# First layer: another order inside the convolutions' copies, and a PSUM count that starts anew after every merged stretch

## The chip, the cores and the metric

The kernel runs on one core of a Trainium2 chip. The time is device time in microseconds (us) of that core. The engines have short names in what follows: PE is TensorE (matrix products and transposes; PEld its weight loads), DVE is VectorE, ACT is ScalarE, POOL is GpSimd, and SP issues most of the data transfers (DMA). PE writes its results to PSUM, a memory of eight banks of 2 KiB per partition; DVE and ACT read them from there and write to SBUF, the on-chip working memory.

## The reference

The input x is a float32 tensor of shape 8 x 56 x 56 x 192 (image, row, column, channel). Four layers follow one another, each of the form x = x + layer(groupnorm(x)). The last three (a pooled attention with nine-point windows, a gated attention in 8 x 8 windows, and a linear recurrence along rows, columns and diagonals) are not touched by the change. The first layer is:

```python
p = silu(x @ p_w.T + p_b); q = silu(x @ q_w.T + q_b); v = silu(x @ v_w.T + v_b)   # 192 -> 576 channels
qv = q * v
o1 = toeplitz(qv, a1)             # along the columns of each row, per channel
o2 = toeplitz(transpose(qv), a2)  # along the rows of each column, per channel
out = (p * (o1 + o2)) @ o_w.T + o_b
```

A toeplitz product is, for each of the 576 channels, a 56 x 56 matrix built from one sequence of coefficients, applied to each row (or column) of the image.

## The kernel before

`layer0` handles the eight images one after the other. The 576 channels are nine heads of 64, named by s. Two heads make a chunk, named by c: chunks 0 to 3 hold two heads each and chunk 4, the tail, holds one. For one chunk:

- **Gates and products** (`project`, gates at L358, silu at L369): four steps g compute q and v for a quarter of the image each. A step takes two PSUM tiles, or one in the tail chunk. ACT applies silu, and DVE and POOL multiply q and v into the tile `qv` (L381, L387), once row by row and once column by column.
- **Turns** (`turn_both`, L414 and L419; `turn` for the tail head, L433 and L440): PE transposes qv for eight image rows into one PSUM tile. DVE copies one half of it to one operand (`ol`), and after that ACT copies the other half to the other operand (`or`). A pair of heads has seven turns, the tail head four.
- **Convolutions** (`convolve`, L457): two steps q per head. A step runs 32 matrix products, one per channel, whose operands hold both the Toeplitz tables and the turned qv, so that one product gives o1 + o2 for a channel. Its PSUM tile has two banks (k); each holds eight channels (v) of 56 image rows (h), and the partitions hold image columns, for two channel groups at once (u). One copy per step moves it to `ot`, a tile of 120 partitions x 56 rows x 128 channels, by DVE when q is 0 (L477) and by ACT when q is 1 (L475). The tail head has its own two copies (L468).
- **Post** (`post`, for chunks 0 and 1 and for chunks 2 and 3; `post_tail` for chunk 4): computes p, transposes `ot` back (L518), multiplies (L523), applies the output weights (L532, L553, L564) and adds to the image's accumulators `acca` and `accb` (L484, L486). Its tile `o` is taken by name (`outs`), apart from the ring.

PE's order is fixed by the program: the layer opens a manual schedule for PE. The other engines are ordered by the scheduler that builds the program, and each runs its own queue in order.

**The ring of PSUM tiles.** All eight banks belong to tiles of two banks: three tiles with the tag `c` and one with the tag `o`. Every step asks `banks()` for a tile. In wide mode each fourth request, by the running count `ring["at"]`, gets `o` and the others get the next of the three `c`; in narrow mode all requests get `c` and the count stands still. A request must wait until the readers of the tile's previous user are done.

**The loop over chunks.** For each chunk c, `merge` interleaves two lists. One is the previous post (if there is one) or, when there is none, the gates of the first two steps of the next chunk; the other is this chunk's turns. Then the remaining gate steps of the next chunk run, beside steps of group normalization where there are any (`normalize` for the next image at c = 2, `tell` for the finished image at c = 1; their statistics go through PE at L129), and then this chunk's convolutions. In chunk 3 gates and convolutions alternate. The posts therefore fall into the merges of c = 2 and c = 4 (narrow), and the tail's post into that of c = 0 of the next image (wide). After a convolution the tables of the head after next are loaded by DMA into the operand that it has freed (`toeplitz`, L334; in the first image from the freshly built coefficients, later from a stored copy).

Of the kernel before, what the change touches and what calls it, by code (L numbers as in the profile page):

```python
# [17 lines left out]
H = 56  # L18
# [40 lines left out]
def image_dma(queue, dram, xa, xb, store=False):  # L59


    parts = []
    for at in range(0, HW, HQ // 2):
        cols = slice(at, at + HQ // 2)
        parts.append((xa[0:CP, cols], dram[:, 0, cols]))
        parts.append((xa[CP:CA, cols], dram[0 : CA - CP, 1, cols]))
        h, own = at // HQ, slice(at % HQ, at % HQ + HQ // 2)
        parts.append((xb[h * CB : (h + 1) * CB, own], dram[CA - CP :, 1, cols]))
    for s, d in parts:
        if store:  # L70
            queue.dma_start(d, s)
        else:
            queue.dma_start(s, d)
# [104 lines left out]
def layer0(cx, xin, xout, w, consts):  # L178
# [15 lines left out]
    with ExitStack() as es:  # L194
# [7 lines left out]
        ring = {"at": 0, "wide": True}  # L202

        def banks():
            if ring["wide"]:
                ring["at"] += 1
                if ring["at"] % 4 == 0:
                    return cx.tile(psc, [128, 2, 512], "o", bufs=1)
            return cx.tile(psc, [128, 2, 512], "c")
# [17 lines left out]
        def fetch_wqv(q, queue=nc.sync):  # L227
            if q < B * NC:
                wqv[q] = cx.tile(cp, [128, 3, 2, 128], "wqv", bufs=2)
                queue.dma_start(wqv[q], w["w_qv"][q % NC])  # L230

        def fetch_wp(j, queue=nc.sync):
            wps[j] = cx.tile(cp, [128, 3, 2, 128], "wp")
            queue.dma_start(wps[j], w["w_p"][j])
# [8 lines left out]
        with ExitStack() as pes:  # L243
# [22 lines left out]
            for t in (1, 2):  # L266
# [13 lines left out]
                for i in range(3):  # L280
                    ps = banks()[0:32, 0, 0:NP]
# [4 lines left out]
                for s in range(NS):  # L286
                    ps = banks()[0:DS, 0, 0:NP]
# [116 lines left out]
        def turn_both(n):  # L404

            order = (n % 2, 1 - n % 2)

            def step(i0):
                ps = banks()[0:120]
                view = ps.rearrange("p k (d i) -> p k d i", i=8)  # L410
                for i in range(8):
                    for e, k in enumerate(order):
                        rows = slice(e * DS, (e + 1) * DS)
                        nc.tensor.transpose(  # L414
                            view[:, k, :, i], qv[rows, i0 + i, :], ident[rows, rows]
                        )
                for t, rows, copy in zip(both, (T2, T1), (nc.vector.tensor_copy, nc.scalar.copy)):
                    dst = t[rows, :, 0:ND].rearrange("p k (d i) -> p k d i", i=H)
                    copy(dst[:, :, :, i0 : i0 + 8], view[rows])  # L419

            return [lambda i0=i0: step(i0) for i0 in range(0, H, 8)]

        def turn(n):

            s = n % NS
            e = s % 2 * DS
            left, right = pairs[n % 2]

            def step(i0, ni):
                ps = banks()[0:120]  # L430
                view = lambda k: ps[:, k].rearrange("p (d i) -> p d i", i=8)
                for i in range(ni):
                    nc.tensor.transpose(  # L433
                        view(i // 8)[:, :, i % 8], qv[e : e + DS, i0 + i, :],
                        ident[e : e + DS, e : e + DS],
                    )
                src = ps[:, 0 : ni // 8].rearrange("p k (d i) -> p d k i", i=8)
                for t, rows, copy in ((left, T2, nc.vector.tensor_copy), (right, T1, nc.scalar.copy)):
                    dst = channels(t)[rows, :, i0 : i0 + ni].rearrange("p d (k i) -> p d k i", i=8)
                    copy(dst, src[rows])  # L440

            return [lambda i0=i0: step(i0, min(16, H - i0)) for i0 in range(0, H, 16)]

        def convolve(n, ot):


            s = n % NS
            left, right = pairs[n % 2]
            tail = s == NS - 1

            def step(q):
                ps = banks()
                for k in range(2):
                    for v in range(8):
                        for u in range(2):
                            d = q * 16 + 8 * k + v + u * 32
                            nc.tensor.matmul(  # L457
                                ps[u * 64 : (u + 1) * 64, k, v * H : (v + 1) * H],
                                left[:, d * H : d * H + 64],
                                right[:, d * H : (d + 1) * H],  # L460
                                start=True, stop=True, skip_group_check=True,
                            )
                if tail:
                    for u, copy in enumerate((nc.vector.tensor_copy, nc.scalar.copy)):
                        d0 = q * 16 + u * 32
                        dst = ot[0:H, :, d0 : d0 + 16].rearrange("p h (k v) -> p h k v", k=2)
                        src = ps[u * 64 : u * 64 + H, :, 0 : 8 * H]
                        copy(dst, src.rearrange("p k (v h) -> p h k v", h=H))  # L468
                    return
                else:  # L470
                    d0 = s % 4 * 32 + 16 * q
                    dst = ot[:, :, d0 : d0 + 16].rearrange("p h (k v) -> p k v h", k=2)
                    src = ps[0:120, :, 0 : 8 * H].rearrange("p k (v h) -> p k v h", h=H)
                if q % 2:
                    nc.scalar.copy(dst, src)  # L475
                else:
                    nc.vector.tensor_copy(dst, src)  # L477

            return [lambda q=q: step(q) for q in range(2)]

        def add(m, j, x, ps):
# [217 lines left out]
        def merge(a, b):  # L699

            n = max(len(a), len(b))
            for i in range(n):
                for x in (a, b):
                    for f in x[-(-i * len(x) // n) : -(-(i + 1) * len(x) // n)]:
                        f()
# [11 lines left out]
        def whole(steps):  # L717
            return [lambda f=f, h=h: (f(), h()) for f, h in steps]
# [3 lines left out]
        for b in range(B):  # L722
            more = b + 1 < B
            for c in range(NC):
                n = b * NS + 2 * c
                two = c < NC - 1
                turns = turn_both(n) if two else turn(n)

                i = b * NC + c
                fetch_wqv(i + 2)  # L730
                ahead = project(xn if two else nxt, i + 1) if two or more else []
                early = [] if fill else ahead[0:2]
                ring["wide"] = c not in (2, 4)
                merge(fill + [f for f, _ in early], turns)
                ring["wide"] = True
                for _, f in early:
                    f()
                ahead = whole(ahead[len(early) :])
                if fill:
                    fetch_wp({2: 1, 4: 2, 0: 0}[c])  # L740
                fill, beside = [], []
                if c == 0:
                    if after is not None:
                        image_dma(nc.sync, xout[b - 1], *after, store=True)
                        beside, telling = tell(b - 1, *after)
                    if more:
                        nxt = load_raw(b + 1)
                if c == 1:
                    acc = new_acc(b)
                    beside = [lambda f=f: f(banks) for f in telling]  # L750
                if c == 2 and more:
                    beside = normalize(nxt)

                if c % 2 == 0:
                    ot = cx.tile(cp, [120, H, 128] if two else [H, H, DS], "ot")
                convs = []
                for m in (n, n + 1) if two else (n,):
                    *some, last = convolve(m, ot)
                    convs += some + [lambda m=m, last=last: (last(), toeplitz(m + 2))]

                if c == NC - 2:
                    k = len(ahead)
                    ahead = [f for pair in zip(ahead, convs[0:k]) for f in pair]
                    convs = convs[k:]
                merge(ahead, beside)
                for f in convs:
                    f()
                if c in (1, 3):
                    fill = post(c // 2, xn, ot, acc)
            fill, after = post_tail(xn, ot, acc), acc  # L770
            xn = nxt
# [1448 lines left out]
```

## Time and profile before

| what | value |
|---|---|
| median of three runs | 4062.7 us (4059.47 to 4067.02) |
| the profiled execution: its own time | 4071.48 us |
| its span, first to last instruction | 4069.7 us |
| PE busy | 3788.5 us (93%) |
| DVE busy | 2415.4 us (59%) |
| ACT busy | 1843.3 us (45%) |
| POOL busy | 1529.7 us (38%) |
| mean granted clock of PE | 0.98 |
| last PE work of the first layer | 1931 us from the start |

The profile is of one execution. A row of a group of instructions gives line, engine, operation, the tiles written and read, the shapes and a count. A row of the timeline gives the start and the length in us, then the engine, line and tiles; what stands in brackets is the idle time of the engine before it, and the instruction whose end released it. A row of the waits gives who waited for whom: total us, number of times, longest. In a table of stretches each engine has its busy time and its number of instructions, followed by the clock granted to PE (1.00 is full), the share of time that the DMA engines were busy, and GB/s. PE's transposes and products follow each other closely, and their recorded lengths overlap.

### The profile page before, as it was taken

To read this page: it belongs to the slowest core of one execution; us is meant where nothing else is said; L and a number is where in the kernel's file an instruction comes from. 1 tells how busy PE (TensorE), PEld (TensorE's weight loads), DVE (VectorE), ACT (ScalarE), POOL (GpSimd) and SP (SyncE) were. 2 spreads that over 40 slices of the span, in tenths; PEclk is the share of its full clock that TensorE was granted. 3 is DMA by queue.
4 is the path that set the end of the run, shared out by engine and by line. 5 is a ranking of instruction groups with operands and counts; after the bars stand their busy time and mean duration, and the time that the engine had idled before them with its cause. 6 is when DMAs were issued, how large, how long until landed. Compare 5 with 4: busy or idle time off the path is not lost.

```text
span 4069.7 us, 115870 instructions
## 1 busy us (share of the span) xinstructions
PE 3788.5 (93%) x51036; PEld 2658.5 (65%) x51036; DVE 2415.4 (59%) x3318; ACT 1843.3 (45%) x2021; POOL 1529.7 (38%) x1325
## 2 busy tenths in 40 slices
PE   6989999999998999999799999899989999998997
PEld 4777767677776767777466666444435555556997
DVE  5557675666657665565544444566656666664664
ACT  2444444344444434444334443343335555553663
POOL 3222242222233222223433333333334445444776
PEclk9999999999999999999899999999999999999999
DMA  7865353423526352342433443556558766663333
GB/s 154 166 137 145 81 141 103 119 76 102 128 76 158 87 134 68 87 112 65 120 99 99 112 100 102 158 167 204 178 152 189 176 153 161 149 141 101 94 103 98
DMA packets 390300, 507.94 MB, mean 125 GB/s; under 512 B 176932, under 2 KB 326724, under 8 KB 388404
## 3 DMA queue, kind: packets, MB, share of 16 engines
q1 hardware_dynamic: 385621, 494.07, 47.9%
q8 instruction: 401, 6.57, 0.7%
q10 hardware_dynamic: 3135, 3.47, 0.3%
q0 software_dynamic: 1040, 2.99, 0.3%
q14 instruction: 103, 0.84, 0.1%
HBM read 344.69 MB, written 155.65 MB: 123 GB/s over the span
## 4 chain that ended last, share of the span: by engine, by line
PE 68%; DVE 11%; issue 7%; ACT 5%; DMA 4%; POOL 3%; SPq 2%; POOLq 0%; DVEq 0%; ACTq 0%
PE c L358 9%; PE h L2053 6%; PE v L1541 6%; PE c L499 6%; PE o L532 4%; PE c L1060 4%; PE c L457 4%; PE y L1095 3%; PE o L358 3%; PE kv L1601 3%; DVE ol L419 2%; PE c L1066 2%; PE c L1763 2%; PE c L553 2%; PE o L457 1%
## 5 line engine op out<-in xcount | busy, mean ns | idle before, releaser
L387 POOL TENSOR_TENSOR qv<-s,s 128x392 f32<-128x392 f32 (+3 forms) x320 | 574.7, 1824 | 1296.0 <-ACT s L369 1033.9
L358 PE MATMUL c<-x,wqv 64*128 64x392 f32 x2556 | 458.1, 503 | 21.5 <-DVE ot L477 7.0
L358 PEld LDWEIGHTS c<-x,wqv 64*128 64x128 f32 x2556 | 249.7, 190 | 179.6 <-issue 9.6
L369 ACT ACTIVATE s<-c,bqv 128x784 f32<-128x784 f32 (+1 forms) x235 | 213.6, 914 | 258.3 <-PE c L358 240.9
L381 DVE TENSOR_TENSOR qv<-s,s 128x784 f32<-128x784 f32 (+1 forms) x160 | 232.8, 1465 | 128.5 <-ACT s L369 128.5
L499 PE MATMUL c<-x,wp 64*128 64x224 f32 x2688 | 284.1, 357 | 15.3 <-ACT s L506 14.5
L419 DVE COPY ol<-c 56x1024 f32<-56x1024 f32 x183 | 217.5, 1209 | 105.0 <-PE c L414 105.0
L499 PEld LDWEIGHTS c<-x,wp 64*128 64x128 f32 x2688 | 256.2, 190 | 19.8 <-ACT s L506 16.7
L419 ACT COPY or<-c 56x1024 f32<-56x1024 f32 x183 | 182.7, 1008 | 170.9 <-DVE ol L419 164.9
L523 DVE TENSOR_TENSOR s<-s,c 128x896 f32<-128x896 f32 x112 | 121.8, 1088 | 231.3 <-ACT s L506 224.9
L457 PEld LDWEIGHTS c<-or,ol 120*64 120x64 f32 x6912 | 217.0, 143 | 30.8 <-issue 23.3
L457 PE MATMUL c<-or,ol 120*64 120x56 f32 x6912 | 224.5, 227 | 11.5 <-issue 6.7
L1552 ACT ACTIVATE vb<-sm 128x1024 f32<-128x1024 f32 (+1 forms) x100 | 103.9, 1040 | 261.7 <-issue 218.1
L2084 POOL TENSOR_TENSOR y<-y,s 128x448 f32<-128x448 f32 x168 | 185.2, 1103 | 90.1 <-ACT s L2063 90.1
L506 ACT ACTIVATE s<-c,bp 128x448 f32<-128x448 f32 x224 | 129.9, 631 | 179.6 <-PE c L499 178.3
L2053 PE MATMUL h<-ringv,am 128*64 128x57 f32 (+1 forms) x4400 | 192.6, 235 | 17.6 <-DVE ringv L2040 10.6
L1541 PE MATMUL v<-wvb,wa 128*128 128x512 f32 (+1 forms) x400 | 191.9, 612 | 6.1 <-ACT wa L1427 6.1
L2053 PE MATMUL h<-ringh,am 128*64 128x57 f32 (+1 forms) x4400 | 186.1, 231 | 8.1 <-DVE ringh L2059 8.1
L2053 PEld LDWEIGHTS h<-ringv,am 128*64 128x64 f32 x4400 | 168.1, 140 | 20.9 <-DVE ringv L2040 11.5
L358 PE MATMUL o<-x,wqv 64*128 64x392 f32 x900 | 165.2, 497 | 13.2 <-DVE ot L477 2.8
L1060 PE MATMUL c<-wv,xc 128*126 128x192 f32 x896 | 175.7, 339 | 0.5 <-issue 0.5
L2053 PEld LDWEIGHTS h<-ringh,am 128*64 128x64 f32 x4400 | 166.1, 139 | 10.4 <-DVE ringh L2059 10.4
(273 smaller groups left out, 7853.6 us busy)
## 6 DMA issues: line engine op xcount, KB each, us to landing
or<-tt SPq DMA_DIRECT2D x252, 196.0 KB
ol<-tt SPq DMA_DIRECT2D x252, 196.0 KB
vt<-v SPq DMA_DIRECT2D x56, 672.0 KB
v<-vb SPq DMA_DIRECT2D x96, 384.0 KB
x<-x SPq DMA_DIRECT2D x110, 168.0 KB
wqv<-in_l_w_qv SPq DMA_DIRECT2D x38, 384.0 KB
x<-in_x SPq DMA_DIRECT2D x64, 196.0 KB
x<-x SPq DMA_DIRECT2D x110, 112.0 KB
```

The lines of the kernel that those rows point to most:

```text
L358: nc.tensor.matmul(ps[:, h, 0:n], wqv[q][rows, k, i, :], xn[rows, k, g * n : (g + 1) * n], start=(k == 0), stop=(k == 2),)
L369: nc.scalar.activation(t, ps[rows, :, 0:n], AF.Silu, bias=bqv[rows, j : j + 1])
L381: nc.vector.tensor_tensor(sub(qv[rows, 7 * g :, 64 + H - 1 :], (HH * 120, 2), (120, 7), (-1, H)), *(t.rearrange("p u (h w) -> p u h w", w= ...
L387: eng.tensor_tensor(sub(qv[rows, w0:, H - 1 - 7 * g - HH * u :], (120, w1 - w0), (-1, 7)), *(t[:, u].rearrange("p (h w) -> p w h", w=H)[:, ...
L419: copy(dst[:, :, :, i0 : i0 + 8], view[rows])
L457: nc.tensor.matmul(ps[u * 64 : (u + 1) * 64, k, v * H : (v + 1) * H], left[:, d * H : d * H + 64], right[:, d * H : (d + 1) * H], start=Tr ...
L499: nc.tensor.matmul(ps[:, h, u * n : (u + 1) * n], wps[j][rows, k, u, :], xn[rows, k, g * n : (g + 1) * n], start=(u == 0 and k == 0), stop ...
L532: nc.tensor.matmul(outs[q][:, h, i * n : (i + 1) * n], wo[rows, 2 * j + u, 0:CA], gated[g][rows, u, h * n : (h + 1) * n], start=(i == 0 an ...
L1060: nc.tensor.matmul(out(i, u), group(i, u), wv[0], start=(u == 0), stop=True, skip_group_check=True,)
L1541: nc.tensor.matmul(out, x[:, at : at + n], wt, start=(k == 0), stop=(k == 1), skip_group_check=True,)
L2053: nc.tensor.matmul(ps[sides[c], y], am[a][:, m * CB : (m + 1) * CB], old[:, x], start=(n < 2), stop=True, skip_group_check=True,)
L2084: nc.gpsimd.tensor_tensor(v, v, line[:, j], ALU.add)
```

## The change

Two edits, both in the first layer.

In `convolve`, the copy from PSUM to `ot` of the heads other than the tail visits the same 896 elements per partition in another order. Before, the order from outside to inside was bank k, channel v, image row h: the innermost step goes through consecutive words of PSUM and through `ot` in steps of a whole row of 128 channels. Now it is h, k, v: the innermost 16 elements are consecutive words of `ot`, and PSUM is read in steps of 56 words. The dimension that the code names h is the outer one, and the 16 channels are the inner ones, as in the tail's copies.

In the loop over chunks, the line behind `merge` put the ring back into wide mode. Now it sets the running count to zero as well, so that the next three requests get `c` and the fourth gets `o`. The line stands in the loop over all chunks and so runs behind each merge.

```diff
                     d0 = s % 4 * 32 + 16 * q
-                    dst = ot[:, :, d0 : d0 + 16].rearrange("p h (k v) -> p k v h", k=2)
-                    src = ps[0:120, :, 0 : 8 * H].rearrange("p k (v h) -> p k v h", h=H)
+                    dst = ot[:, :, d0 : d0 + 16].rearrange("p h (k v) -> p h k v", k=2)
+                    src = ps[0:120, :, 0 : 8 * H].rearrange("p k (v h) -> p h k v", h=H)
...
                 ring["wide"] = c not in (2, 4)
                 merge(fill + [f for f, _ in early], turns)
-                ring["wide"] = True
+                ring.update(at=0, wide=True)
```

## The prediction

> **What bounds the kernel now.** I read the page first (busy rows, chain), then the stretches of the first layer, which ends near 1931 us, and then every wait of TensorE (PE) there. The chain that ended last is 68% PE. A steady image (990 to 1220 us) keeps PE busy 214.9 of 230 us, VectorE (DVE) 148.8 and ScalarE (ACT) 106.9, so an edit counts only through PE's 15 idle us per image.
>
> The view of one line's instructions gives the edited copies (L475, L477), and the last head's copies (L468), which already go columns outside, channels inside (ns: min/median/max):
>
> ```profile
> L475 ACT COPY ot<-c x48: 1653/1737/1826, 95.5 to 1875.7; 120x896 f32<-120x896 f32 x48
> L477 DVE COPY ot<-c x49: 1633/1711/1792, 97.4 to 1876.6; 120x896 f32<-120x896 f32 x49
> L468 DVE COPY ot<-c x11: 1071/1075/1083, 297.4 to 1918.6; 56x896 f32<-56x896 f32 x11
> L468 ACT COPY ot<-c x11: 902/902/904, 298.5 to 1919.7; 56x896 f32<-56x896 f32 x11
> ```
>
> Same 896 elements per partition, two thirds and half of the time. Whom PE waits for in the first layer (total us, times, longest):
>
> ```profile
> PE c L358 <- DVE ot L477: 7.0, 5, 1.4
> PE o L358 <- DVE ot L477: 2.8, 2, 1.4
> PE o L358 <- DVE acca L484: 2.5, 2, 1.3
> PE o L358 <- DVE acca L486: 2.4, 2, 1.2
> ```
>
> The first two rows are all that the edited copies cost PE directly, bar 1.3 us at L518. The last two are what a restart right behind a post can remove.
>
> **Part 1, the copies.** 128 of them, half on each engine. From the L468 row I take 1.08 us on DVE (saves 0.64) and 0.90 on ACT (saves 0.84): 41 us of DVE and 53 of ACT. Almost all lies beside PE work. In the timeline where chunk 3 begins:
>
> ```profile
> 1147.49 3.17 DVE L477 COPY ot<-c 120x896 f32<-120x896 f32 x2
> 1149.18 2.25 PE L358 MATMUL c<-x,wqv 64*128 64x392 f32 x12 [1.39 <-DVE ot L477]
> ```
>
> PE needs the tile of the first of these two copies, so it starts one saving, 0.64 us, earlier. Seven images show this; in the first, a later 7.7 us wait for the tables' DMA (230 us) swallows it: 6 x 0.64 = 3.8 us. Where the post then reads ot, PE waits 0.3 us for DVE's last copy in four images; that goes: 1.2 us. **Sum -5.0.** At the other boundary with a post (1077 us) ACT's copy ends at 1079.16, but its table load waits for PE's gates until 1079.97: nothing there. The cover of the rest is the 2 us that each gate or convolution step takes on PE; without it 128 savings would be 94 us.
>
> [...] the old form writes every 4-byte element 512 B further on. [...] The new copy reads PSUM in steps of 56 floats. Were that as slow for a copy, the -5.0 would be 0. The L468 row reads in just that step at 1.08 us, so I use the row; between ends of 0.90 and 1.74 us per copy it is by far the nearest.
>
> **Part 2, the count behind a post.** L735 sets the count to zero after every merge, not only those with a post. Behind a post (c = 2, 4) the first tile is now c, never the o whose last add is still running. From the waits above: 2.5 + 2.4 = **-4.9 us**, four of 16 posts. After it the fourth tile is o, which is the order of one image today (1121 us), with no wait.
>
> **Part 3, the count behind the other merges.** In wide mode the order is c c c o, so each allocation reuses the tile of four allocations before. If the count restarts at remainder r, the next r allocations of c reuse the tile of three before. From the code: c = 1 has 8 gate + 4 convolution tiles since the last restart, then 4 + 7: 23, r = 3. c = 0: 8 + 2, then 10 + 7: 27, r = 3. c = 3: 8 + 2 + 4, then 2 + 7: 23, r = 3. All three get shallower by one tile, just where PE has run ahead of the turn copies. The timeline at c = 1:
>
> ```profile
> 1055.96 1.01 ACT L419 COPY or<-c 56x1024 f32<-56x1024 f32 x1 [0.41 <-DVE ol L419]
> 1057.02 2.25 PE L358 MATMUL c<-x,wqv 64*128 64x392 f32 x12 [0.73 <-ACT or L419]
> 1057.09 1.01 ACT L419 COPY or<-o 56x1024 f32<-56x1024 f32 x1
> ```
>
> PE now waits for the fourth-last turn (free at 1056.97). It will wait for the third-last, free at 1058.10: 1.1 us later. Behind it on PE stand this gate and the statistics matmuls; DVE's chain waits for those, but stands in its own work until 1062.48, 0.4 us after them, so the later wait at L129 takes 0.35 back: +0.75. In the first image the table DMA at 126 us swallows it. 7 x 0.75 = 5.2.
>
> At c = 0:
>
> ```profile
> 1016.53 1.01 DVE L486 TENSOR_TENSOR accb<-c,accb 128x392 f32<-128x392 f32 x2
> 1016.74 2.19 PE L358 MATMUL o<-x,wqv 64*128 64x392 f32 x12
> 1018.71 2.14 ACT L419 COPY or<-c 56x1024 f32<-56x1024 f32 x2 [2.54 <-DVE ol L419]
> ```
>
> The gate at 1016.74 has today's o. It will take the c that DVE reads until 1017.54: start 1017.60, +0.86; its second tile waits for the turn copy ending at 1019.72, +0.12. Seven images: +7.0. Behind it stand seven gate tiles, whose products POOL finishes at 1034.8, 14 us before the transposes that need them (1048.6), so nobody adds to this.
>
> At c = 3 the gate moves from 1159.40 to 1160.31 (the next turn copy ends at 1160.26). The convolution behind it waits until 1162.13 for the last turn's data anyway, so of 0.9 only 0.25 is left (estimate from these times): 7 x 0.25 = 1.8. **Sum +14.0.** No DMA is added or moved; SP's table loads follow the convolutions, by at most these amounts, and the image loads land as before.
>
> **Part 4, TensorE's clock.** The stretches around a stall:
>
> ```profile
> 1065.02:1068.43 3.41, 2.32 (x32) 1.57 (x30) 3.02 (x4) 2.30 (x3) 3.41 (x3) 1.00 0.33 97
> 1068.43:1071.85 3.42, 3.42 (x72) 3.42 (x68) 3.39 (x4) 0.29 (x1) 3.42 (x3) 0.50 0.06 23
> ```
>
> PE idles 1.1 us and runs tiny statistics matmuls for another; for the next 3.41 us the granted clock (third column from the end) is 0.50, and 1.7 us are lost. [...] The trace trips it with PE busy 2.32 of 3.41 us, so the row decides. Today's c = 3 stall pair (1.17 and 0.35 us) is followed by half clock in three of seven images. New: 1.85 us at c = 1; 1.39 and 0.86 at c = 0; 1.17 and 1.25 at c = 3. Between none and all 21 places (36 us) I take two more windows net, since the c = 1 statistics stall shrinks and 1.4 us waits trip nothing today: **+3.4**.
>
> **Sum:** -5.0 - 4.9 + 14.0 + 3.4 = **+7.5 us**. The profiled execution took 4071.5 (span 4069.7); it becomes 4079. The three runs' median lies 8.8 below it, so **4070 us**.
>
> **Rivals.**
> 1. *The clock turns the new waits into a loss.* Slower: with half clock at 8 to 10 of the new stalls instead of 2, +10 to +14: 4080 to 4084. For it: the c = 0 pair leaves PE under half busy in 2.8 us. Against it: near 1014 us PE idles about as long today at full clock. From three extra windows on it is a measurable loss.
> 2. *The shallower ring doesn't bite.* If DVE and ACT issue in another order once copies are shorter, turn copies come out earlier and PE's waits are absorbed: -5.0 - 4.9 and no more: 4053. For it: DVE sat idle 2.7 us at 1141.6 with the first ot copy ready. Against: the turn copies at 1055 us run back to back already.
> 3. *The copies stay slow* [...]: +12.5, 4075.
>
> **How the numbers follow.** About 0.2% (8 us) is what a measurement here can tell. The forecast has 0.50 (own range 4064 to 4077; 0.32 of it within 0.2%, 0.18 slower), rival 1 0.18 (slower), rival 2, whole or in part, 0.25 (0.17 faster, 0.08 within), rival 3 0.07 (0.05 slower, 0.02 within). Faster 0.17, same 0.42, slower 0.41. Range for 8 in 10: 4052 (rival 2) to 4084 (rival 1).
>
> **What would show it.** Copies at L475/L477 near 0.90 and 1.08 us; no PE wait for acca at L358; PE's wait for turn copies after c = 1 near 1.85 us, a new wait for accb at c = 0, the wait at chunk 3's start near 0.75; about two more half-clock stretches in the first layer than the 15 of today. Waits at c = 0 and 1 as today would make the prediction wrong towards faster; many half-clock stretches towards slower.

## The result, and the profile after

The changed kernel takes 4065.3 us where the kernel before, on the same chip, takes 4061.1: ratio 1.0010, 95% interval 0.9998 to 1.0021. That alone can't be told from no change. A second comparison (below) gives 1.0017, interval 1.0007 to 1.0027. So the change costs about 4 to 7 us. Its profiled execution took 4069.0 us, with a span of 4067.2.

The copies became as short as forecast. One line's instructions, changed kernel (ns: min/median/max):

```profile
L475 ACT COPY ot<-c x32: 905/905/909, 93.1 to 1870.8; 120x896 f32<-120x896 f32 x32
L477 DVE COPY ot<-c x64: 1027/1080/1093, 94.9 to 1871.7; 120x896 f32<-120x896 f32 x64
```

With the 32 copies of ACT from `o` (906 ns), the busy rows fall by 44 us on DVE (2415.4 to 2371.5) and 54 on ACT (1843.3 to 1789.6). PE is as busy as before (3786.1 for 3788.5). What became of that is in PE's waits in the first layer (total us, times, longest), first of the changed kernel:

```profile
PE c L358 <- ACT or L419: 24.7, 17, 1.9
PE c L358 <- DVE ot L477: 5.8, 7, 0.8
PE c L358 <- PE c L414: 5.2, 7, 0.7
PE c L499 <- ACT or L440: 2.5, 8, 0.3
PE c L129 <- DVE dev L165: 1.0, 1, 1.0
```

then, of the rows that change most, three of the kernel before:

```profile
PE c L358 <- ACT or L419: 6.7, 13, 0.7
PE o L358 <- ACT or L419: 2.2, 4, 0.7
PE c L129 <- DVE dev L165: 5.5, 5, 1.1
```

The two waits for `acca` are gone. The waits for DVE's copies fell from 9.8 us (7.0 + 2.8) to 5.8. But the waits of the gates for turn copies, 6.7 + 2.2 us before, are now 24.7, and 5.2 us stand in a row that wasn't there. The waits of the statistics (L129), 8.8 us before with two rows not shown (2.2 and 1.1), are down to 1.0. Where they lie is seen in the timeline of the same steady image (start, length, then engine, line and tiles; in brackets the idle time before).

Behind c = 0:

```profile
1014.10 1.01 DVE L486 TENSOR_TENSOR accb<-c,accb 128x392 f32<-128x392 f32 x2
1015.22 6.01 PE L358 MATMUL c<-x,wqv 64*128 64x392 f32 x34 [0.74 <-PE c L414]
```

The view names L414 as releaser, but that work had long been done. What ends at 1015.11 is the add to `accb` from the tile that the gate takes: the wait that the forecast put here.

The 0.74 us in brackets are less than the wait costs: idle time is counted from the recorded end of the transposes, which overlaps the next product (in the kernel before the last turn below is recorded to 1016.90, and the gate starts at 1016.74). So the cost is read from start to start, from the last turn to the first convolution, before and (last two rows) after:

```profile
1016.22 0.68 PE L414 MATMUL c<-ident,qv 64*120 64x64 f32 x16 [1.39 <-ACT or L419]
1032.68 2.08 PE L457 MATMUL o<-or,ol 120*64 120x56 f32 x64
1013.79 0.68 PE L414 MATMUL c<-ident,qv 64*120 64x64 f32 x16 [1.39 <-ACT or L419]
1031.37 4.87 PE L457 MATMUL c<-or,ol 120*64 120x56 f32 x158
```

That is 16.47 us before, in all seven images, and 17.57 after, in the five that run at full clock here: 1.10 us more. (The nanoseconds of the trace give these; the rounded rows give 16.46 and 17.58.)

Behind c = 1 the changed kernel has (POOL's rows are from a view of POOL alone; both are the same timeline):

```profile
1056.65 4.22 PE L358 MATMUL c<-x,wqv 64*128 64x392 f32 x24 [1.86 <-ACT or L419]
1060.70 0.95 PE L129 MATMUL c<-mean,gmat 64*128 64x1 f32 x16
1061.70 0.16 DVE L137 COPY spread<-c 128x2 f32<-128x2 f32 x1 [0.72 <-PE c L129]
1062.09 0.37 DVE L163 TENSOR_TENSOR dev<-mean,spread 128x2 f32<-128x2 f32 x1
1062.49 1.51 DVE L164 TENSOR_TENSOR dev<-dev 128x2 f32<-128x2 f32 x1
1064.04 1.52 DVE L165 TENSOR_TENSOR dev<-dev,mv 128x2 f32<-128x2 f32 x1
1065.70 1.06 PE L129 MATMUL c<-dev,gmat 64*128 64x1 f32 x16
1060.12 2.32 POOL L387 TENSOR_TENSOR qv<-s,s 128x392 f32<-128x392 f32 x1
1062.40 1.58 POOL L387 TENSOR_TENSOR qv<-s,s 128x392 f32<-128x392 f32 x1
1063.95 1.59 POOL L387 TENSOR_TENSOR qv<-s,s 128x392 f32<-128x392 f32 x1
```

and the kernel before has, for the same steps:

```profile
1062.78 1.17 DVE L163 TENSOR_TENSOR dev<-mean,spread 128x2 f32<-128x2 f32 x1
1063.99 1.52 DVE L164 TENSOR_TENSOR dev<-dev 128x2 f32<-128x2 f32 x1
1065.54 1.49 DVE L165 TENSOR_TENSOR dev<-dev,mv 128x2 f32<-128x2 f32 x1
1067.18 1.06 PE L129 MATMUL o<-dev,gmat 64*128 64x1 f32 x16 [1.09 <-ACT s L369]
1061.60 3.89 POOL L387 TENSOR_TENSOR qv<-s,s 128x392 f32<-128x392 f32 x2
1065.44 1.58 POOL L387 TENSOR_TENSOR qv<-s,s 128x392 f32<-128x392 f32 x1
```

The wait in front of the gates is 1.86 us instead of 0.73, as forecast. But the second statistics step, for which PE waited 1.09 us before, no longer waits at all. From the end of the turns (1054.79, and 1056.29 before) to the convolution at L457 (1066.69, and 1068.16) it is 11.90 us now and was 11.87: the image loses 0.03 us.

The rows of DVE and POOL show why. Three DVE instructions of two elements per partition (L163 to L165) each end 0.01 to 0.02 us after an instruction of POOL: now at 1062.46, 1064.00 and 1065.56 against POOL's 1062.44, 1063.98 and 1065.54; before, L164 and L165 ended at 1065.51 and 1067.03 against 1065.49 and 1067.02. L137, which reads PSUM, takes 0.16 us. Where no product of POOL runs, the same three instructions in the kernel before are short:

```profile
2024.49 0.16 DVE L163 TENSOR_TENSOR dev<-mean,spread 128x2 f32<-128x2 f32 x1
2024.68 0.16 DVE L164 TENSOR_TENSOR dev<-dev 128x2 f32<-128x2 f32 x1
2024.88 0.16 DVE L165 TENSOR_TENSOR dev<-dev,mv 128x2 f32<-128x2 f32 x1
```

So POOL's products, not DVE's own work, pace this chain. POOL starts them 0.18 us behind the end of the turns in both kernels (1054.97 and 1056.47), and the chain ends 10.77 us behind the turns now and 10.74 before, whether the gates came early or late. These ends coincide in the whole of both profiled executions: the 70 instructions of L163 to L165 that began beside a product of POOL each ended 0.01 to 0.02 us after the end of one and took 0.20 to 1.53 us; the 26 that began beside none took 0.15 to 0.16 us. L163 to L165 read SBUF alone. L137 and L138 read PSUM, and the 109 of them that began beside a product of POOL took 0.14 to 0.16 us.

Behind c = 3, after and (second fence) before:

```profile
1156.74 3.83 PE L358 MATMUL c<-x,wqv 64*128 64x392 f32 x12 [1.25 <-ACT or L419]
1160.49 1.68 PE L457 MATMUL c<-or,ol 120*64 120x56 f32 x48
```

```profile
1159.40 2.25 PE L358 MATMUL o<-x,wqv 64*128 64x392 f32 x12 [0.35 <-ACT or L419]
1162.13 2.15 PE L457 MATMUL c<-or,ol 120*64 120x56 f32 x64 [0.49 <-ACT or L419]
```

The gate waits 0.90 us more and the convolution 0.49 less. What is left is again read from start to start, from the last turn to the second convolution step behind it: 8.02 us before (1158.37 to 1166.39), and in an image of the changed kernel at full clock

```profile
686.48 0.69 PE L414 MATMUL c<-ident,qv 64*120 64x64 f32 x16 [1.17 <-ACT s L369]
694.78 2.08 PE L457 MATMUL o<-or,ol 120*64 120x56 f32 x64
```

8.30, so 0.28 us more. The gate of the image above now takes 3.83 us instead of 2.25: the clock. Two of the stretches of the changed kernel, each with the one before it (busy us of PE, PEld, DVE, ACT and POOL, then granted clock, DMA share, GB/s):

```profile
307.38:310.79 3.41, 1.28 (x26) 0.92 (x22) 3.41 (x7) 1.01 (x1) 0.00 (x0) 0.99 0.39 103
310.79:314.20 3.41, 3.41 (x14) 2.15 (x12) 3.41 (x6) 2.01 (x2) 0.00 (x0) 0.51 0.83 231
450.70:454.10 3.40, 0.97 (x20) 0.81 (x20) 3.40 (x4) 3.36 (x5) 1.35 (x1) 1.00 0.43 109
454.10:457.50 3.40, 3.40 (x12) 1.42 (x10) 3.38 (x3) 1.51 (x2) 3.40 (x3) 0.50 0.00 0
```

The first pair is at c = 0 (waits of 1.38 and 0.74 us), the second at c = 3 (1.17 and 1.25). In each of the two, one stretch holds both waits, PE is busy for 1.28 and 0.97 of its 3.4 us, and the clock of the next stretch is 0.51 and 0.50.

### The profile page after: what moved, and what is told of

The parts are those of the page before. It is cut to its first block, busy times and chain, and to the rows that moved or that the text cites. A ratio compares the mean times of both kernels' runs of the same rounds, so it can differ in the third digit from the quotient of the medians.

```text
span 4067.2 us, 115859 instructions
## 1 busy us (share of the span) xinstructions
PE 3786.1 (93%) x51036; PEld 2655.7 (65%) x51036; DVE 2371.5 (58%) x3318; ACT 1789.6 (44%) x2021; POOL 1523.3 (37%) x1325
## 5 line engine op out<-in xcount | busy, mean ns | idle before, releaser
L358 PE MATMUL c<-x,wqv 64*128 64x392 f32 x2856 | 518.3, 509 | 45.9 <-ACT or L419 24.7
L358 PEld LDWEIGHTS c<-x,wqv 64*128 64x128 f32 x2856 | 285.0, 193 | 223.6 <-ACT or L419 29.8
L369 ACT ACTIVATE s<-c,bqv 128x784 f32<-128x784 f32 (+1 forms) x270 | 244.9, 913 | 330.0 <-PE c L358 308.1
L499 PE MATMUL c<-x,wp 64*128 64x224 f32 x2688 | 282.1, 356 | 17.0 <-ACT s L506 14.4
L499 PEld LDWEIGHTS c<-x,wp 64*128 64x128 f32 x2688 | 254.5, 189 | 21.7 <-ACT s L506 16.6
L457 PEld LDWEIGHTS c<-or,ol 120*64 120x64 f32 x7168 | 217.3, 139 | 40.4 <-issue 38.0
L457 PE MATMUL c<-or,ol 120*64 120x56 f32 x7168 | 225.3, 224 | 19.3 <-issue 10.1
L1570 POOL TENSOR_TENSOR l<-vb,ta 128x512 f32<-128x512 f32 (+1 forms) x52 | 75.2, 1446 | 259.5 <-ACT vb L1552 258.5
```

What stands on the lines that cost most here:

```text
L358: nc.tensor.matmul(ps[:, h, 0:n], wqv[q][rows, k, i, :], xn[rows, k, g * n : (g + 1) * n], start=(k == 0), stop=(k == 2),)
L369: nc.scalar.activation(t, ps[rows, :, 0:n], AF.Silu, bias=bqv[rows, j : j + 1])
L457: nc.tensor.matmul(ps[u * 64 : (u + 1) * 64, k, v * H : (v + 1) * H], left[:, d * H : d * H + 64], right[:, d * H : (d + 1) * H], start=Tr ...
L499: nc.tensor.matmul(ps[:, h, u * n : (u + 1) * n], wps[j][rows, k, u, :], xn[rows, k, g * n : (g + 1) * n], start=(u == 0 and k == 0), stop ...
```

## The experiments

My theory at this point: the copies and the restart behind the posts gain, the restart behind c = 0 and c = 3 loses, by its waits and by the clock, and the one behind c = 1 is given back. The rivals: a restart costs its own waits only (no clock), and the c = 1 term costs what was forecast. The first three diffs below are against the kernel before, the later ones against the third, which has the new copies and restarts the count only behind the posts. All ratios are to the kernel before, measured on the same chip; 0.1% is 4.1 us.

**The copies alone.** The diff's first part only, with the count as it was.

```diff
-                    dst = ot[:, :, d0 : d0 + 16].rearrange("p h (k v) -> p k v h", k=2)
-                    src = ps[0:120, :, 0 : 8 * H].rearrange("p k (v h) -> p k v h", h=H)
+                    dst = ot[:, :, d0 : d0 + 16].rearrange("p h (k v) -> p h k v", k=2)
+                    src = ps[0:120, :, 0 : 8 * H].rearrange("p k (v h) -> p h k v", h=H)
```

> The new copies, the count left to run on as before. Theory (few waits of TensorE end at these copies, so 94 us of saved VectorE and ScalarE time are worth little): copies near 1.08 and 0.90 us; the wait at chunk 3's start 0.8 us instead of 1.4 in six images; the four waits for acca at 1.2 us stay; the waits behind c = 0, 1, 3 stay as before (0.73 at c = 1, 0.35 at c = 3, none at c = 0). -4 us against before, 0.1%. Rival (the copies give the engines slack that TensorE profits from elsewhere): clearly more, -10 us or better. Rival (a PSUM read in steps is slow): copies near 1.7 us, 0 us.

Measured: 4061.3 us, ratio 0.9992 (0.9982 to 1.0002), -3 us. The wait at chunk 3's start is 0.77 us, the waits at c = 1 and c = 3 are as before, and so are those for `acca`. Its waits also show where the 1.2 us at the post went:

```profile
PE c L499 <- ACT or L440: 2.5, 8, 0.3
```

The wait for the last copy at L518 (1.3 us in all before) is gone, but this one, 0.6 us in two images before, is now there in all eight. PE reaches its next wait that much earlier: from the first gate of this post to its last products (L532) it is 39.12 us, before and now. So the copies give what PE waits for at chunk 3, and 98 us less of DVE and ACT work give no more.

**The restart alone.** The diff's second part only, with the old copies.

```diff
-                ring["wide"] = True
+                ring.update(at=0, wide=True)
```

> The restart after every merge alone, with the old copies. Theory (it takes one tile of depth behind c = 0, 1 and 3, and only the restart behind the posts gives something): the waits of TensorE as in the changed kernel, 0.71 us for the tile that accb is read from at c = 0, 1.86 at c = 1, 1.25 at c = 3; no wait for acca; 1.4 us at chunk 3's start. 5.0 + 0.4 + 3 - 4.9 = +3 to +4 us, plus 0 to +4 from the half clock: 4 to 8 us slower than before. Rival (the restart is worth nothing either way): 0.

Measured: 4085.4 us, ratio 1.0048 (1.0029 to 1.0066), +20 us, and this was a miss: two and a half to five times the loss expected. Its waits do not account for it:

```profile
PE c L358 <- ACT or L419: 24.3, 17, 1.9
PE c L358 <- DVE ot L477: 9.3, 7, 1.4
PE c L358 <- PE c L414: 5.2, 7, 0.7
```

They are those of the changed kernel, and 3.5 us more at chunk 3's start. What differs is the clock: 20 windows (of 3.41 us) at half clock in the first layer, against 15 in the changed kernel. Every run has its mean granted clock on record, and one less that clock, times the span, is taken as the time lost to it: 92.5 us on average here, 76.9 in the 34 runs of the kernel before. These 15.7 us (standard error 3.3) and 3.4 us of waits (the terms for `acca`, c = 0 and c = 3 in the last table) come to 19 of the 20.

**The restart only behind the posts.** New copies, and:

```diff
                 ring["wide"] = True
+                if c in (2, 4):
+                    ring["at"] = 0
```

> The new copies and the restart only behind the two posts (c = 2 and 4). Theory: both gains without the shallower ring: no wait for acca, 0.8 us at chunk 3's start, the waits at c = 0, 1 and 3 as before the change (none, 0.73, 0.35). -4 - 5 = -9 us against before, 0.2%, and 13 us faster than the changed kernel. Rival (the restart behind c = 0, 1, 3 cost nothing, the loss is chance in the half clock): as the changed kernel, +4 us.

Measured: 4052.7 us, ratio 0.9968 (0.9957 to 0.9980), -13 us. Read from start to start, its two gains are worth 9.4 us (in the last table), which the interval, 8 to 17, holds. Its waits at the gates and statistics:

```profile
PE o L129 <- ACT s L369: 7.7, 7, 1.1
PE c L358 <- ACT or L419: 7.0, 10, 0.9
PE c L358 <- DVE ot L477: 5.3, 7, 0.9
```

No wait for `acca` or `accb`, and the waits at c = 1 and c = 3 at their old depth. So the three other restarts hold the whole loss. The next three runs put them back.

**Behind c = 0 too.**

```diff
-                if c in (2, 4):
+                if c in (0, 2, 4):
```

> New copies, restart behind the posts and behind c = 0. Theory: seven new waits of 0.71 us where a gate takes the tile that accb is read from, all of them on TensorE's path: 5 us above the restart behind the posts only, -7 to -8 us against before. Rival (the whole loss sits at c = 1, where the wait grew most): as behind the posts only, -12 us.

Measured: 4060.9 us, ratio 0.9995 (0.9985 to 1.0006). That is 0.27% or 11 us above the restart behind the posts alone, with an interval of about 6 us to each side. The wait for `accb` is back with its 5.2 us:

```profile
PE c L358 <- PE c L414: 5.2, 7, 0.7
```

But from the last turn to the convolution the five images at full clock take 17.57 us for 16.47, as in the changed kernel, so in seven images the wait costs 7.7 us and not 5; two more half-clock stretches (below) would be 3.4.

**Behind c = 3 too.**

```diff
-                if c in (2, 4):
+                if c in (2, 3, 4):
```

> New copies, restart behind the posts and behind c = 3. Theory: the gate there waits 1.25 instead of 0.34 us, and the convolution behind it no longer 0.49 us: 0.4 us per image, 3 us, and up to 5 more if the pair of waits of 1.17 and 1.25 us halves the clock more often: 3 to 8 us above the restart behind the posts only, -5 to -9 us against before. Rival (the loss sits at c = 1 alone): -12 us.

Measured: 4055.6 us, ratio 0.9989 (0.9975 to 1.0004), 0.21% or 8.5 us above the posts alone, again with a wide interval (some 7 us to each side).

```profile
PE c L358 <- ACT or L419: 15.8, 17, 1.3
```

The row grew by 8.8 us over that of the posts alone, the 0.9 us at each gate and some 2.4 us that stood in a row of `o`. At full clock 0.28 us per image are left of it, as in the changed kernel. The rest is the clock: 82.0 us lost to it on average, 5.7 more than in the kernel before (standard error 1.8).

**Behind c = 1 too.** First alone beside the posts:

```diff
-                if c in (2, 4):
+                if c in (1, 2, 4):
```

> New copies, restart behind the posts and behind c = 1. Theory (the longer wait at c = 1, 1.86 instead of 0.73 us, is given back by the wait for the statistics at L129, 1.06 us, which goes): 0 to 1 us above the restart behind the posts only, -12 us against before; the L129 waits of 1.06 us absent from the trace. Rival (it is not given back): 8 us above it, -4 us against before.

Measured: 4045.2 us, ratio 0.9960 (0.9948 to 0.9972). The time alone would have told for "given back", but the trace shows that the test was empty:

```profile
PE c L358 <- ACT or L419: 6.8, 10, 0.7
PE c L129 <- DVE dev L165: 6.8, 8, 1.0
```

The longest wait of a gate is still 0.7 us and the statistics wait is still there. Without a restart behind c = 0, there are 27 + 23 = 50 requests between the restart behind c = 4 and that behind c = 1: remainder 2. Then the first request behind the merge still gets the tile of four before; only the second and third get shallower, and PE doesn't wait for those. So the term needed c = 0 in:

```diff
-                if c in (2, 4):
+                if c in (0, 1, 2, 4):
```

> New copies; the count restarts behind c = 0, 1, 2 and 4. The last run with a restart behind c = 1 kept the 0.73 us wait there: without the restart behind c = 0 the count stands at another remainder at c = 1, so that it made no step shallower and tells nothing of this term. With c = 0 in, the remainder is 3 as in the changed kernel. Both theories expect the wait of 1.86 us there in seven or eight images. Theory (given back): the statistics waits at L129 (about 1.1 us in seven images) go, so that the first layer without its clock loss is as long as with c = 0, 2, 4 alone, 1845 us within 2; ratio to the kernel before 0.998 to 1.0015. Rival (the prediction's own term): of the added 1.1 us only 0.35 come back at L129, 5 us more: first layer about 1850, L129 keeps about 0.7 us per image.

Measured: 4060.6 us, ratio 1.0004 (0.9992 to 1.0016), inside the range of "given back", and within its interval of the kernel with c = 0, 2 and 4 (0.9995). With the clock's scatter the time can't separate 0 from 5 us, but the waits do:

```profile
PE c L358 <- ACT or L419: 15.9, 10, 1.9
PE c L129 <- DVE dev L165: 1.0, 1, 1.0
```

The wait of 1.86 us is there, and of the statistics waits, 8.7 us with c = 0 alone, 1.0 is left: 7.7 us, or 1.1 per image, against the 0.35 of the rival. From the last turn to the convolution of chunk 1 it is 12.57 to 12.59 us at full clock (five images), and 12.54 to 12.57 with c = 0, 2 and 4. The first layer from its first gate on, less half of its time at half clock, is 1844.5 us long, and 1844.9 there. So the term is given back.

**The changed kernel again**, without an edit.

> The changed kernel once more, beside the three that restart at one more place than the posts. Theory: the restart behind c = 0, 1 and 3 costs waits of 5.0 + 0.4 + 3 us and some half clock: +0.1% against before, 10 to 13 us above the kernel that restarts behind the posts only (which was 12.5 below before).

Measured: 4068.8 us, ratio 1.0017 (1.0007 to 1.0027).

**The restart alone again**, to see whether its +20 was chance.

> Old copies, the count restarts behind every merge, a second time. Its first time (1.0048 of before) was 16 us above the changed kernel, though its trace, without the clock loss, was only 2 us longer. Theory (draws of the clock): the copies are worth 4 us here as they were beside the old count, so this gives 4070 to 4074, ratio 1.002 to 1.004. Rival (slow copies and a restarted count cost more together): again 1.0045 or more.

Measured: 4073.7 us, ratio 1.0036 (1.0021 to 1.0052), +15 us, with 24 windows at half clock. This lies inside the range of the first theory; the interval reaches into the rival's as well. So part of the first +20 was chance, but the copies seem worth more beside the restarted count (8 to 16 us) than beside the old one (3 us). The difference is clock: 11.7 us more are lost to it here than in the kernel before (standard error 2.6) and 15.7 the first time, but 4.8 in the changed kernel (1.5). The windows of the traces point the same way (20 and 24, against 15 and 14). Why old copies should bring more of them isn't settled.

**DVE's copies alone in the new order.** Restart behind the posts; ACT's copies as before.

```diff
-                    dst = ot[:, :, d0 : d0 + 16].rearrange("p h (k v) -> p h k v", k=2)
-                    src = ps[0:120, :, 0 : 8 * H].rearrange("p k (v h) -> p h k v", h=H)
+                    order = "p k v h" if q % 2 else "p h k v"
+                    dst = ot[:, :, d0 : d0 + 16].rearrange("p h (k v) -> " + order, k=2)
+                    src = ps[0:120, :, 0 : 8 * H].rearrange("p k (v h) -> " + order, h=H)
```

> Restart behind c = 2 and 4; the new order in DVE's copies alone, ACT's keep the old one (1.74 us). Theory: PE waits for DVE's copies only, so ACT's 0.84 us per copy are worth nothing: ratio 0.996 to 0.998 as with both copies new, and the wait at chunk 3's start stays near 0.85. Rival: ACT's shorter copies let its turn copies come earlier and are worth a few us: ratio 0.998 to 0.9995.

Measured: 4047.9 us, ratio 0.9973 (0.9964 to 0.9982), as with both copies new (0.9968), and the wait at chunk 3's start is unchanged (5.2 us in seven). ACT's 54 us are worth nothing that can be measured.

**Which stride is priced.** Restart behind the posts; the copies' innermost two elements now lie a bank apart in PSUM and eight words apart in `ot`.

```diff
-                    dst = ot[:, :, d0 : d0 + 16].rearrange("p h (k v) -> p h k v", k=2)
-                    src = ps[0:120, :, 0 : 8 * H].rearrange("p k (v h) -> p h k v", h=H)
+                    dst = ot[:, :, d0 : d0 + 16].rearrange("p h (k v) -> p h v k", k=2)
+                    src = ps[0:120, :, 0 : 8 * H].rearrange("p k (v h) -> p h v k", h=H)
```

> Restart behind c = 2 and 4; copies ordered row, channel, bank from outside to inside: the innermost two elements lie a bank (512 words) apart in PSUM and eight words apart in ot. Which side of a strided copy is priced? If the destination's step alone counts, each write lands within the same 64 bytes and the copies stay near 0.90 and 1.08 us. If any step other than one word in the destination costs, they return to 1.71 and 1.74. If PSUM's step counts once it changes bank, they are slower than 1.1 too; the two last are not told apart by this run.

Measured once: 4054.6 us. The copies:

```profile
L475 ACT COPY ot<-c x48: 1652/1726/1811, 92.4 to 1863.9; 120x896 f32<-120x896 f32 x48
L477 DVE COPY ot<-c x49: 1636/1709/1784, 94.3 to 1864.8; 120x896 f32<-120x896 f32 x49
```

They are back at the price of the old order (1.74 and 1.71 us), though each group of 16 elements stays within 64 bytes of `ot`. So here it wasn't enough to write near the last element. Whether the step of eight words in `ot` or the hop between banks brought the price back, this run doesn't tell.

**A version that beats both.** With the posts' restarts, PE's largest wait for DVE at a gate is at chunk 3's start (0.85 us), where the copies of chunk 2's convolutions stand behind the products of the last gate step. In chunks 0 to 2 these products are issued one convolution step later:

```diff
-                ahead = whole(ahead[len(early) :])
+                ahead = ahead[len(early) :]
+                held = None
+                if c in (0, 1, 2) and ahead:
+                    ahead[-1], held = (ahead[-1][0], lambda: None), ahead[-1][1]
+                ahead = whole(ahead)
...
                 merge(ahead, beside)
+                if held is not None:
+                    convs.insert(1, held)
```

> As the kernel with the restart behind posts only, and in chunks 0 to 2 the products of the last gate step are issued behind the first convolution step, so that VectorE copies that step's result before it multiplies. Theory (at chunk 3's start TensorE waits because VectorE does the products first, not because its copy is long): the 0.8 us wait there goes, in seven images: another -5 us, -14 us against before. Rival (the wait moves: the later products hold the transposes of the next chunk): the same time as the kernel it starts from, or slower.

Measured: 4047.6 us, ratio 0.9955 (0.9937 to 0.9973), -18 us, below the kernel before and the changed one. From the posts' restarts alone (0.9968) the time doesn't tell it apart. The waits at L358 for DVE's copies are gone; for turn copies, PE's transposes wait a little more than with the posts' restarts alone (14.3 us for 12.1, the longest 2.2).

**Half clock, by the place of the stall before it.** In the traces of the kernel before and of the changed kernel, 26 of the 29 stretches at half clock in the first layer lasted 3.41 us (two others 6.83, one 10.24), so one is counted as 1.7 us lost. How often one followed a stall of each place in the first layer, from the 14 profiled executions:

| place | restart acts there | stretches in each trace | mean | in the other traces | mean |
|---|---|---|---|---|---|
| c = 0 | changed kernel (2 traces), restart alone (2), c = 0 (1), c = 0, 1 (1) | 2, 1, 2, 2, 2, 3 | 2.0 | 0 in all eight | 0 |
| c = 1 (gate's wait, or the statistics') | changed (2), restart alone (2), c = 0, 1 | 2, 3, 4, 5, 2 | 3.2 | 3, 3, 3, 3, 1, 2, 3, 2, 3 | 2.6 |
| c = 3 | changed (2), restart alone (2), c = 3 | 5, 3, 6, 6, 4 | 4.8 | 3, 2, 1, 0, 1, 0, 3, 1, 0 | 1.2 |

In windows this is +2.0 at c = 0, +0.6 at c = 1 and +3.6 at c = 3: 6.2, or 10.5 us. The place explains the means. In which image a stretch comes differs from trace to trace: in the trace of either kernel the starts of the stretches lie whole multiples of 3.41 us apart, within 0.01 us. Cut into such cells, the changed kernel's trace has the pair of c = 3 in one cell in five images, with PE busy for 0.97 to 1.42 us, and half clock followed all five; in the image at 686.48 two cells share the pair (2.50 and 1.90 us busy), and full clock stayed. At c = 0 half clock followed cells with 1.28 and 1.80 us busy, and none of those with 2.02 to 2.67. By the 14 traces, all 60 cells from the layer's first gate on in which PE was busy for less than 1.25 us were followed by half clock, whatever the place, and 10 of the 6921 in which it was busy for over 2.5. It was otherwise ahead of that gate: nine cells with less than 1.25 us in the trace of either kernel were followed by full clock. That the stretches differ from trace to trace fits the scatter of the kernel before, 4053 to 4067 us over 12 executions.

## Why the prediction was right, and where not

The forecast was 4070 us, +7.5 to the kernel before, in 4052 to 4084. Measured were +4 and +7 beside the kernel before: the sum was right. The range alone says little, since it holds the kernel before as well (4061). The terms are measured from the start of one PE instruction to that of another, at full clock, where an interval repeats within about 0.05 us from image to image; the clock's term is from the mean clocks of 22 runs and of 55 of the kernel before on the same chip.

| step of the prediction | forecast | measured |
|---|---|---|
| Part 1: chunk 3's start | -3.8 | -3.4 (11.17 to 10.60 us from chunk 2's convolutions to the turns, six images) |
| Part 1: the post's reading of `ot` | -1.2 | 0 (39.12 us from the post's first gate to its last products, before and after) |
| Part 2: waits for `acca` | -4.9 | -6.0 (from the post's last products to the next convolution: 2 x 1.52 and 2 x 1.47) |
| Part 3: c = 0 | +7.0 | +7.7 (7 x 1.10, from the last turn to the convolution) |
| Part 3: c = 1 | +5.2 | 0 (12.57 to 12.58 us, from the last turn to the convolution) |
| Part 3: c = 3 | +1.8 | +1.7 (6 x 0.28) |
| Part 4: the clock | +3.4 | +4.8 (81.1 us lost for 76.3, standard error 1.5) |
| sum | +7.5 | +4.8 |

- **The copies** fell to the row I had taken, 1.08 and 0.90 us, while reading PSUM in steps of 56 words. The cover held too: all that came back is what PE waits for. The 1.2 us at the post is the step that failed here: I stopped at the wait that goes, and didn't look at the next one, the 0.32 us that a gate of the post (L499) then waits for the tail's last turn.
- **Behind the posts** no wait for `acca` came back. Restart and copies together gained 13 us, with an interval from 8 to 17, where parts 1 and 2 had 9.9 and the table has 9.4.
- **At c = 0** mechanism and size were right: a new wait for `accb`. The gate starts 1.43 us behind the last turn's start (1013.79 to 1015.22) instead of 0.52, so 0.91 later where 0.86 was forecast, and 1.10 are lost with what follows, where 0.98 was. The waits' row, 5.2 us in all, shows too little.
- **At c = 1** the step that failed is "the later wait at L129 takes 0.35 back": it takes back all 1.1, so the 5.2 us forecast here are 0. I took DVE's own work for what holds the chain ("DVE's chain ... stands in its own work until 1062.48"). It is POOL's products that pace it, and those start 0.18 us behind the end of the turns, before the gate's wait ends.
- **At c = 3** the gate waits 1.25 us as foretold, and 0.28 us is left per image where 0.25 was forecast.
- **The clock** was right in its sum, within its error, but not in its places. I had dismissed c = 0 since waits of 1.4 us tripped nothing; with the new wait beside it the pair trips in two images of seven. At c = 3 the pair of 1.17 and 1.25 trips in nearly five of eight. By the counts at these places alone the term would be the 10.5 us above; over all runs the clock shows 4.8, and what makes up the difference is open. Rival 1's 10 to 14 us on top of the forecast are not there.

Without the two terms that failed, c = 1 and the post, the forecast would have been +3.5, which the measured +4 to +7 allow as well as +7.5: the time alone could not have shown these two steps wrong. Rivals 2 (the ring doesn't bite) and 3 (slow copies, a guess that no trace backed) fell with the traces. The forecast of two more half-clock stretches than 15 is not seen in the changed kernel's own trace, which has 14. Those behind the stalls of c = 0, c = 1, c = 3 and the post rose from 9 to 11, but the others, behind waits for DMA or such as the view puts down to nothing ("issue", 2 to 3.3 us), fell from 6 to 3. One trace is too few for a count that scatters so.

## What to carry to other kernels

Restarting a rotating count is not neutral: each restart at remainder r makes up to r later requests one tile shallower, so do it only where the tile that it avoids is the busy one; here that is behind the posts, and those two restarts with the new copies gain 0.3% where restarting everywhere loses 0.1 to 0.2%. Read what a wait costs from start to start, since idle time by recorded ends showed 0.74 us of 1.10 here. Before adding up waits, follow each lost microsecond to the next thing that PE waits for, and ask what paces that: if it doesn't start later for the stall (POOL's products here), the stall costs next to nothing (0.03 us here, of 1.1). Count two short waits that stand close together as one: here half clock followed all five pairs of 1.17 and 1.25 us that lay in one stretch of 3.41 us.

## What the runs showed of the hardware

- **DVE's end beside POOL's products.** DVE operations on 128 x 2 elements that read SBUF alone took 0.20 to 1.53 us where they began beside a POOL product, and ended within 0.02 us of the end of one (all 70 in two traces). Where they began beside none they took 0.15 to 0.16 us (26), and operations of this size that read PSUM took 0.14 to 0.16 us beside POOL's products (109).
- **Half clock, and PE's work before it.** In the changed kernel's first layer 13 of 14 stretches at half clock followed 3.41 us in which PE was busy for 0.97 to 1.80 us, and one followed 3.41 us without PE work. In the kernel before, all 15 followed 3.41 us with 0.44 to 2.32 us of PE work. There the pair of 1.17 and 0.35 us left PE busy for 1.90 us of 3.41 in two images alike: half clock followed at 686.14, full clock at 1157.18.
- **A copy's price by the steps of its reads and writes.** 896 elements per partition from PSUM took 1.08 us (DVE) and 0.91 (ACT) with consecutive words written and steps of 56 words read; they took 1.71 and 1.74 with consecutive words read and steps of 128 words written, and 1.71 and 1.73 with steps of eight words written and of a bank read.
